# Graph layers on one core: exponents of the ranked layer overwrite their masks, and elementwise work is placed by an estimate of each engine's backlog

## Chip, core and metric

The kernel runs on one core of a Trainium2 chip. The metric is the time of one execution on the device, in microseconds (us). Five engines run side by side, each with its own queue of instructions that it works off in order: TensorE (PE, matrix products), VectorE (DVE), ScalarE (ACT), GpSimd (POOL) and SyncE (SP, here only for issuing DMAs). PEld is TensorE's loading of weights.

## What is computed

Node features x (3327 x 64) pass four layers with one sparse weighted adjacency matrix adj (3327 x 3327); each layer adds its result to x. Cut to what matters:

```python
def layer0(h):                       # twice: k = 0, 1
    m = adj @ (x @ W); gi = m @ wih.T + bih; gh = x @ whh.T + bhh
    r = sigmoid(i_r + h_r); z = sigmoid(i_z + h_z); n = tanh(i_n + r * h_n)
    return relu((1 - z) * n + z * x)
def layer1(h):                       # k = 2, the ranked layer
    mask = (adj != 0); rank = cumsum(mask, axis=1); deg = rank[:, -1:]
    kk = minimum(deg, 100); pos = rank - (deg - kk)
    w = mask * where(pos > 0, 0.5 ** (kk - pos), 0)
    return w @ (h @ weight) + bias
def layer2(h):                       # k = 3, 4, 5, the squared ones: w = adj * adj
    for W, b in ...: x = (w @ x) @ W.T + b
def layer3(h):                       # k = 6, 7
    for W in ...: x = tanh(concat([adj @ x, x]) @ W)
# each layer: h = relu(layernorm(x)); x = x + layer(h)
```

## The kernel before

**Products.** There are eight passes over the adjacency matrix, k = 0 to 7 (KIND, line 69: plain, plain, ranked, squared three times, plain twice). The nodes are laid out in two halves of 13 blocks of 128, both halves side by side (64 features each) in the 128 rows of a result. The 13 blocks make four chunks of destination nodes, of 384, 384, 384 and 512 columns, and two groups: group 0 is chunks 0 and 1, group 1 is chunks 2 and 3. A tile is the strip of the transposed matrix of one block of 128 sources and one group: 2 x 768 or 2 x 896 float32 columns, 768 or 896 KB. There are 26 tiles to a group, and they are loaded again for each pair of passes, 234 loads in all (L296 on SP), into NBUF = 20 slots of the on-chip memory.

A unit is (k, chunk, tile): the product of one tile's columns of one chunk with the source block's features y[k], two matmuls side by side (one per half), summed in a bank of PSUM (propagate, L488). In the timeline a float32 unit of 384 columns takes 0.64 us. A ranked unit has bf16 exponents against three bf16 terms of y, so three pairs of matmuls.

**Order.** alone and joint write the list of units (there are 888): joint(g, k) lays pass k of group g and pass k+1 of the same tiles into each other, so that a tile loaded once serves both. In joint(0, 1) the second pass lies 20 tiles behind. The list is not touched by the change. By units: 208 to 263 hold pass 1 of group 0, 250 to 313 the ranked pass of group 0, 314 to 389 that of group 1, with pass 3 (squared in place in the slot) laid in from 326 on.

run (L593) walks this list once and writes out the program of every engine: it issues loads up to 60 units ahead while slots are free (reserve of 3), calls prepare up to PREPARE units ahead, calls expand two units ahead, then propagate. take and give hand out PSUM banks: four for sums, four for everything else.

**The ranked layer.** For each tile a mask (adj != 0, bf16) is written by DVE in two pieces, one per half (L354), into half a slot (class Mask, two masks to a slot). The mask's last row is replaced by the counts behind this block, by a small DMA that POOL issues (L359). The slot of the tile is free again once the mask is made and pass k = 1 has used it. A product with a triangle of constants (tri, L202) then gives each entry's rank as the exponent of a power of two, in PSUM; an eviction turns it into the bits of a bf16 number: on ACT (L404) or on DVE (L402), by a rule of tile, half and group. The exponents land in a tile "e" of three buffers, in expand, two units before use. Counting units (k = -1, L424) in pass 0 give the counts; their masks are made the same way.

**Tasks.** What follows a chunk's last unit of a pass is a generator: evacuation of the sums (L627 on ACT or L629 on DVE), GRU gates (L703 to L721), transposes, residual (L683), layernorm (L664 to L679, with one power on POOL, L675), splitting in three terms (in_three, L742 and L744, then small DMAs on POOL, L751). Each yield names a planned time; spend, called by each unit with its own planned time, counts it down and resumes the generator. finish runs a generator to its end at once. more_constants is such a task, too: it loads weights, builds block-diagonal ones (L147) and multiplies two of them together (L175 to L182). In after_1, evacuation, the relu of the GRU and the layernorm's square are put on ACT (busy=True).

**Squares.** square (L329) sends two of three to ACT (L331), the others to DVE (L333); for passes 3 and 4 in place, up to 6 units ahead, for pass 5 into half a slot at expansion.

Of the kernel before, what the change touches and what calls it, by code (L numbers as in the profile page):

```python
# [14 lines left out]
AX = mybir.AxisListType  # L15

# [27 lines left out]
P = 128  # L44
# [26 lines left out]
NBUF = 20  # L71
LOAD = 60
PREPARE = {COUNT: 6, PLAIN: 6, RANKED: 44, SQUARED: 6}
EXPAND = 2
RESERVE = 3
SPECIAL = None
# [12 lines left out]
def kernel(  # L89
# [9 lines left out]
    nc = tc.nc  # L99

# [35 lines left out]
    def more_constants():  # L136
# [8 lines left out]
        for h in range(2):  # L145
            hs = slice(h * D, (h + 1) * D)
            nc.vector.tensor_copy(bd[hs, :, hs], packed[hs])  # L147
# [14 lines left out]
        for i, (bi, bh) in enumerate(((BI1, BH1), (BI2, BH2))):  # L162
            nc.vector.tensor_add(bsum[:, i], bcol[:, bi:bi + 2], bcol[:, bh:bh + 2])

        nc.vector.tensor_scalar(wide[0:D], wide[0:D], bcol[0:D, BL1:BL1 + 1], None, op0=ALU.add)
# [3 lines left out]
        nc.vector.tensor_copy(brow[:, 3], ps[:, :D])  # L169
        give(i)  # L170

        for wt, ih in ((W1, IH1), (W2, IH2)):
# [4 lines left out]
            nc.scalar.copy(tr, ps[:, :P])  # L177
# [4 lines left out]
            nc.vector.tensor_copy(bd[:, ih:ih + 3, :].rearrange("p g f -> p (g f)"), ps[:, :3 * P])  # L182
# [14 lines left out]
    def mm(out, lhsT, rhs, start=True, stop=True):  # L197


        for h in range(2):  # L200
            hs = slice(h * D, (h + 1) * D)
            nc.tensor.matmul(out[hs], lhsT[:, hs], rhs, start=start, stop=stop)  # L202

# [40 lines left out]
    def advance(c):  # L244
        running.add(c)
        try:
            tasks[c][1] = next(tasks[c][0])
# [32 lines left out]
    class Tile:  # L280

        def __init__(self, q, g, in_place, early=False):
            self.q, self.g, self.in_place, self.early, self.uses = q, g, in_place, early, 0
            self.b0 = CH[GROUPS[g][0]][0]
            self.w = sum(width(c) for c in GROUPS[g])
            self.slot = self.mask = None
            self.squares = set()
# [5 lines left out]
        def load(self):  # L293
            self.slot = dead.popleft()
# [15 lines left out]
    class Mask:  # L310

        def __init__(self, w):
# [6 lines left out]
            self.view = both[:, h * 2 * GWM:h * 2 * GWM + 2 * w].rearrange("p (s w) -> p s w", s=2)  # L319

# [8 lines left out]
    def square(sq, v, turn):  # L329
        if turn % 3:  # L330
            nc.scalar.activation(sq, v, AF.Square)  # L331
        else:
            nc.vector.tensor_tensor(sq, v, v, ALU.mult)  # L333

    def prepare(k, c, t):

        if t is SPECIAL:
            return
        kind = KIND[k] if k != COUNT else COUNT
        if kind in (RANKED, COUNT) and t.mask is None:  # L340
            make_mask(t, kind)
        if kind == SQUARED and t.in_place and c not in t.squares:
            t.squares.add(c)
            square(t.view(c), t.view(c), t.q + c)

    pieces = deque()

    def make_mask(t, kind):

        t.mask = Mask(t.w)  # L350
        rows = P - 1 if kind == RANKED else P

        def piece(half):
            nc.vector.tensor_scalar(t.mask.view[:rows, half], t.view()[:rows, half], 0.0, None, op0=ALU.not_equal)  # L354
            if half == 0 and kind == RANKED:

                for ch in GROUPS[t.g]:
                    finish(("count", ch))
                nc.gpsimd.dma_start(out=t.mask.view[P - 1:P], in_=totals[t.g][t.q:t.q + D + 1:D, :])  # L359
            if half == 1:  # L360
                t.used()

        pieces.extend([(t, 0, piece), (t, 1, piece)])

    def mask_pieces(n=0, t=None):

        while pieces and (n > 0 or any(u is t for u, _, _ in pieces)):
            _, half, piece = pieces.popleft()
            piece(half)
            n -= 1  # L370

    def expand(k, c, t):
# [9 lines left out]
        if KIND[k] == PLAIN or (KIND[k] == SQUARED and t.in_place):  # L382
            return t.view(c)
        if KIND[k] == SQUARED:
            room = Mask(t.w)
# [520 lines left out]
```

## Time and profile before

| | us |
|---|---|
| median of 3 runs | 751.74 |
| lowest, highest | 749.52, 751.97 |
| the profiled execution, its own time | 749.97 |
| its span, first to last instruction | 748.3 |
| PE busy | 706.1 |
| DVE, ACT, POOL busy | 328.5, 239.3, 90.3 |
| evictions of exponents: ACT L404, DVE L402 | 147 x 0.600, 61 x 0.613 |
| mask pieces, DVE L354 | 208 x 0.605 |
| squares: ACT L331, DVE L333 | 138 x 0.887, 70 x 1.021 |
| loads of tiles | 234, 199.7 MB in all |

How to read it: the span lies inside the profiled execution's own time, 1.7 us shorter. A row "out<-in xcount | busy, mean ns" gives the time in which at least one of the group ran and the mean length of one. Matmuls overlap in pairs, so the mean of one is not its share of PE's time. In the slices of section 2 of the page, the span is cut in 40 pieces of 18.7 us, and a digit is the busy share in tenths. A line of waits reads: engine, what waited, for whom, total us, times, longest. L202 is the helper mm, which all dense products, transposes and triangle products share. The granted clock was full in the whole span.

### The profile page before, as it was taken

To read this page: it belongs to the slowest core of one execution; us is meant where nothing else is said; L and a number is where in the kernel's file an instruction comes from. 1 tells how busy PE (TensorE), PEld (TensorE's weight loads), DVE (VectorE), ACT (ScalarE), POOL (GpSimd) and SP (SyncE) were. 2 spreads that over 40 slices of the span, in tenths; PEclk is the share of its full clock that TensorE was granted. 3 is DMA by queue.
4 is the path that set the end of the run, shared out by engine and by line. 5 is a ranking of instruction groups with operands and counts; after the bars stand their busy time and mean duration, and the time that the engine had idled before them with its cause. 6 is when DMAs were issued, how large, how long until landed. Compare 5 with 4: busy or idle time off the path is not lost.

```text
span 748.3 us, 12340 instructions
## 1 busy us (share of the span) xinstructions
PE 706.1 (94%) x5072; PEld 352.8 (47%) x5072; DVE 328.5 (44%) x557; ACT 239.3 (32%) x373; POOL 90.3 (12%) x112
## 2 busy tenths in 40 slices
PE   5979999999988699899899999999999999999997
PEld 2734444343445577555434444334344454344443
DVE  6656646313993877777865113421252510000000
ACT  0002000202135676768659312730055401000000
POOL 4200000001492431312120000000010000000000
PEclk9999999999999999999999999999999999999999
DMA  9999994299486266292699839962977399907990
GB/s 348 401 342 405 405 395 178 85 331 342 133 277 231 100 198 209 89 356 94 217 332 389 313 95 401 405 266 94 385 275 260 140 406 405 395 18 246 397 391 24
DMA packets 67364, 201.54 MB, mean 269 GB/s; under 512 B 6172, under 2 KB 6916, under 8 KB 67308
## 3 DMA queue, kind: packets, MB, share of 16 engines
q1 hardware_dynamic: 64556, 199.70, 72.2%
q8 instruction: 40, 0.66, 0.4%
q10 hardware_dynamic: 576, 0.85, 0.3%
q0 software_dynamic: 2176, 0.20, 0.2%
q14 instruction: 16, 0.13, 0.0%
HBM read 199.68 MB, written 0.85 MB: 268 GB/s over the span
## 4 chain that ended last, share of the span: by engine, by line
PE 49%; DVE 2%; ACT 1%; POOL 1%; issue 0%; ACTq 0%; DVEq 0%; POOLq 0%
PE sum L488 45%; PE temp L202 4%; ACT adj L331 1%; DVE adj L354 1%; POOL st L675 1%; DVE adj L333 0%; DVE y L679 0%; DVE st L664 0%; DVE xs L683 0%; DVE e L402 0%; DVE st L673 0%; DVE t L672 0%; ACT t L627 0%; DVE t L666 0%; DVE xs L839 0%
## 5 line engine op out<-in xcount | busy, mean ns | idle before, releaser
L488 PE MATMUL sum<-adj,y 128*64 128x384 f32 (+1 forms) x2912 | 537.3, 515 | 17.6 <-DVE y L679 9.2
L488 PEld LDWEIGHTS sum<-adj,y 128*64 128x64 f32 x2912 | 214.8, 138 | 277.1 <-issue 240.8
L354 DVE TENSOR_SCALAR adj<-adj 128x768 bf16<-128x768 f32 (+3 forms) x208 | 115.6, 605 | 34.1 <-PE temp L424 29.6
L331 ACT ACTIVATE adj<-adj 128x768 f32<-128x768 f32 (+1 forms) x138 | 112.9, 887 | 52.0 <-PE sum L488 32.4
L333 DVE TENSOR_TENSOR adj<-adj 128x768 f32<-128x768 f32 (+1 forms) x70 | 69.2, 1021 | 54.7 <-DMA adj<-in_adjT 30.2
L404 ACT ACTIVATE e<-temp,bitsb 128x384 int16<-128x384 f32 (+1 forms) x147 | 81.0, 600 | 30.8 <-PE temp L202 11.9
L629 DVE COPY t<-sum 128x384 f32<-128x384 f32 x14 | 7.8, 556 | 181.9 <-PE sum L488 181.9
L488 PE MATMUL sum<-e,adj 128*64 128x384 bf16 (+1 forms) x624 | 73.9, 339 | 4.6 <-DVE e L402 4.3
L202 PE MATMUL temp<-adj,tri 128*64 128x384 bf16 (+1 forms) x416 | 61.0, 341 | 13.2 <-DVE e L402 6.7
L675 POOL TENSOR_TENSOR st<-st,mhalf 128x6 f32<-128x6 f32 (+1 forms) x16 | 27.4, 1712 | 309.6 <-DVE st L674 309.6
L488 PEld LDWEIGHTS <-adj 128*64 128x64 bf16 x624 | 42.7, 110 | 21.3 <-issue 7.4
L402 DVE TENSOR_SCALAR e<-temp 128x384 int16<-128x384 f32 (+1 forms) x61 | 37.2, 613 | 29.8 <-PE temp L202 22.6
L627 ACT COPY t<-sum 128x384 f32<-128x384 f32 (+1 forms) x18 | 9.5, 527 | 113.0 <-PE sum L488 113.0
L202 PEld LDWEIGHTS <-tri 128*64 128x64 bf16 x416 | 30.6, 109 | 31.0 <-issue 19.1
L359 POOL DMA_DIRECT2D adj<-totals x52 | 31.0, 598 | 115.9 <-DVE adj L354 76.2
L424 PE MATMUL temp<-adj,behind 128*64 128x384 bf16 x208 | 27.7, 339 | 1.7 <-DVE adj L354 1.7
L202 PE MATMUL temp<-bd,t 128*64 128x128 f32 (+1 forms) x320 | 26.1, 279 | 0.4 <-ACT t L627 0.4
L655 ACT COPY hT<-temp 128x384 f32<-128x384 f32 (+1 forms) x12 | 6.1, 506 | 59.2 <-PE temp L202 59.2
L424 PEld LDWEIGHTS <-behind 128*64 128x64 bf16 x208 | 14.2, 110 | 20.5 <-issue 18.2
L202 PEld LDWEIGHTS temp<-bd,t 128*64 128x64 f32 x320 | 19.6, 137 | 7.7 <-issue 3.0
L709 DVE SCALAR_TENSOR_TENSOR adj<-temp,bcol,adj 128x384 f32<-128x384 f32 (+1 forms) x8 | 5.2, 650 | 39.7 <-PE temp L202 34.3
L202 PE MATMUL temp<-t,bd 128*64 128x384 f32 (+1 forms) x96 | 21.1, 517 | 0.1
(74 smaller groups left out, 267.7 us busy)
## 6 DMA issues: line engine op xcount, KB each, us to landing
adj<-in_adjT SPq DMA_DIRECT2D x130, 768.0 KB, 8.4
adj<-in_adjT SPq DMA_DIRECT2D x104, 896.0 KB, 11.0
adj<-in_weights SPq DMA_DIRECT2D x2, 352.0 KB, 15.7
xs<-in_x SPq DMA_DIRECT2D x1, 640.0 KB
out<-xs ACTq DMA_DIRECT2D x3, 192.0 KB
adj<-totals POOLq DMA_DIRECT2D x26, 3.0 KB, 3.2
adj<-totals POOLq DMA_DIRECT2D x26, 3.5 KB, 2.3
out<-xs ACTq DMA_DIRECT2D x1, 256.0 KB, 5.9
```

The lines of the kernel that those rows point to most:

```text
L202: nc.tensor.matmul(out[hs], lhsT[:, hs], rhs, start=start, stop=stop)
L331: nc.scalar.activation(sq, v, AF.Square)
L333: nc.vector.tensor_tensor(sq, v, v, ALU.mult)
L354: nc.vector.tensor_scalar(t.mask.view[:rows, half], t.view()[:rows, half], 0.0, None, op0=ALU.not_equal)
L359: nc.gpsimd.dma_start(out=t.mask.view[P - 1:P], in_=totals[t.g][t.q:t.q + D + 1:D, :])
L402: nc.vector.tensor_scalar(wide[:, s], ps[:, :w], BITS, 0.0, op0=ALU.add, op1=ALU.max)
L404: nc.scalar.activation(wide[:, s], ps[:, :w], AF.Relu, bias=bitsb)
L424: nc.tensor.matmul(counts[c][1][s * D:(s + 1) * D, :w], behind[:, NQ - 1 - t.q:NQ - 1 - t.q + D], t.mask.view[:, s, t.cols(c)], start=firs ...
L488: nc.tensor.matmul(acc[h * D:(h + 1) * D, :w], yq[h], rhs[h], start=first and n == 0, stop=last and n == len(terms) - 1)
L627: nc.scalar.copy(m, acc[1][:, :width(c)])
L629: nc.vector.tensor_copy(m, acc[1][:, :width(c)])
L675: nc.gpsimd.tensor_tensor(st[:, 3, :n], st[:, 2, :n], mhalf[:, :n], ALU.pow)
```

## The change

It does these things:
- Exponents are written over the mask that they come from (weigh), and the mask's half slot is freed after its second ranked unit. The tile "e" is gone, and there are 21 slots.
- Three planned clocks, of PE, DVE and ACT, are kept while the program is written out: each matmul adds to PE's, each elementwise instruction on DVE or ACT adds an estimate to its engine's. The backlog of an engine is how far its clock is ahead of PE's.
- Units up to 56 ahead are put in two lists (enqueue): masks, and ready (exponents and in-place squares). Before each unit, fill makes what is due (counting masks 3 units, ranked masks 9, exponents and squares 4 before use) and, if the backlog allows, one more mask piece and one more entry of ready.
- Squares, exponents and evacuations go to the engine with the smaller backlog.
- A task's planned delay grows by the larger backlog, less 0.6 us.
- In after_1, chunks 2 and 3 (late) have three operations of the GRU and two of the layernorm on POOL; relu and square of chunks 0 and 1 go to DVE.
- after_0 first finishes more_constants.

The other edits (vector and scalar in place of nc.vector and nc.scalar, which only count the time) are left out here:

```diff
-NBUF = 20
+NBUF = 21
 LOAD = 60
-PREPARE = {COUNT: 6, PLAIN: 6, RANKED: 44, SQUARED: 6}
+AHEAD = 56
 EXPAND = 2
 RESERVE = 3
+PE, DVE, ACT = range(3)
...
+    clock = [0.0, 0.0, 0.0]
+    def charge(engine, us):
+        clock[engine] = max(clock[engine], clock[PE]) + us
+    def behind_pe(engine):
+        return max(0.0, clock[engine] - clock[PE])
+    def cost(engine, n, small=False):
+        return 0.2 + 0.00095 * n if engine == ACT else 0.04 + (0.0006 if small else 0.00135) * n
...
+                charge(self.key, cost(self.key, n))
+                return getattr(self.engine, name)(*args, **kw)
...
+        clock[PE] += rhs.shape[1] / 2400 * (1 if rhs.dtype == BF16 else 4)
...
-            tasks[c][1] = next(tasks[c][0])
+            us = next(tasks[c][0])
+            tasks[c][1] = us + max(0.0, max(behind_pe(DVE), behind_pe(ACT)) - 0.6)
...
+            self.slot, self.since = dead.popleft(), clock[PE]
...
-    def square(sq, v, turn):
-        if turn % 3:
-            nc.scalar.activation(sq, v, AF.Square)
+    def square(sq, v):
+        n = v.shape[1] * v.shape[2]
+        if behind_pe(ACT) + cost(ACT, n) < behind_pe(DVE) + cost(DVE, n):
+            scalar.activation(sq, v, AF.Square)
         else:
-            nc.vector.tensor_tensor(sq, v, v, ALU.mult)
-    def prepare(k, c, t):
-        if t is SPECIAL:
+            vector.tensor_tensor(sq, v, v, ALU.mult)
+    masks, ready = [], []
+    def enqueue(j):
+        k, c, t = units[j]
+        if k == COUNT:
+            masks.append((j, t, COUNT))
+        elif t is SPECIAL:
+            pass
+        elif KIND[k] == RANKED:
+            if c == GROUPS[t.g][0]:
+                masks.append((j, t, RANKED))
+            ready.append((j, weigh, c, t))
+        elif KIND[k] == SQUARED and t.in_place and c not in t.squares:
+            t.squares.add(c)
+            ready.append((j, square_in_place, c, t))
+        begun = int(bool(masks) and masks[0][1].mask is not None)
+        masks[begun:] = sorted(masks[begun:], key=lambda m: m[0])
+        ready.sort(key=lambda r: r[0])
+    def mask_piece():
+        _, t, kind = masks[0]
+        if t.mask is None:
+            t.mask = Mask(t.w)
+        half = t.mask.pieces
+        t.mask.pieces += 1
+        rows = P - 1 if kind == RANKED else P
+        charge(DVE, cost(DVE, t.w, small=True))
+        nc.vector.tensor_scalar(t.mask.view[:rows, half], t.view()[:rows, half], 0.0, None, op0=ALU.not_equal)
+        if half == 0 and kind == RANKED:
+            for c in GROUPS[t.g]:
+                finish(("count", c))
+            nc.gpsimd.dma_start(out=t.mask.view[P - 1:P], in_=totals[t.g][t.q:t.q + D + 1:D, :])
+            t.since = clock[PE]
+        if half == 1:
+            t.used()
+            masks.pop(0)
+    def weigh(c, t):
+        if c in t.weights:
             return
-        kind = KIND[k] if k != COUNT else COUNT
-        if kind in (RANKED, COUNT) and t.mask is None:
-            make_mask(t, kind)
-        if kind == SQUARED and t.in_place and c not in t.squares:
-            t.squares.add(c)
-            square(t.view(c), t.view(c), t.q + c)
-    pieces = deque()
-    def make_mask(t, kind):
-        t.mask = Mask(t.w)
-        rows = P - 1 if kind == RANKED else P
-        def piece(half):
-            nc.vector.tensor_scalar(t.mask.view[:rows, half], t.view()[:rows, half], 0.0, None, op0=ALU.not_equal)
-            if half == 0 and kind == RANKED:
-                for ch in GROUPS[t.g]:
-                    finish(("count", ch))
-                nc.gpsimd.dma_start(out=t.mask.view[P - 1:P], in_=totals[t.g][t.q:t.q + D + 1:D, :])
-            if half == 1:
-                t.used()
-        pieces.extend([(t, 0, piece), (t, 1, piece)])
-    def mask_pieces(n=0, t=None):
-        while pieces and (n > 0 or any(u is t for u, _, _ in pieces)):
-            _, half, piece = pieces.popleft()
-            piece(half)
-            n -= 1
+        t.weights.add(c)
+        while t.mask is None or t.mask.pieces < 2:
+            mask_piece()
+        w = width(c)
+        for s in range(2):
+            i, ps = take()
+            v = t.mask.view[:, s, t.cols(c)]
+            mm(ps[:, :w], tri, v)
+            if behind_pe(ACT) + cost(ACT, w) < behind_pe(DVE) + cost(DVE, w) + 0.1:
+                scalar.activation(v.bitcast(I16), ps[:, :w], AF.Relu, bias=bitsb)
+            else:
+                vector.tensor_scalar(v.bitcast(I16), ps[:, :w], BITS, 0.0, op0=ALU.add, op1=ALU.max)
+            give(i)
+        spend(STREAM_US * w / CWM * 0.5)
+    def square_in_place(c, t):
+        while t.ranked and (t.mask is None or t.mask.pieces < 2):
+            mask_piece()
+        square(t.view(c), t.view(c))
+    def make():
+        _, f, c, t = ready.pop(0)
+        f(c, t)
+    def fill(i, loaded):
+        while masks and masks[0][0] <= i + (3 if masks[0][2] == COUNT else 9):
+            mask_piece()
+        while ready and ready[0][0] <= i + 4:
+            make()
+        if masks and masks[0][2] == RANKED:
+            t = masks[0][1]
+            room = t.mask is not None or len(spare) > 0 or len(dead) > (0 if t.uses == 1 else RESERVE)
+            short = loaded < i + 14 and t.uses == 1
+            if room and (short or (behind_pe(DVE) < 0.5 and clock[PE] - t.since > 9.0)):
+                mask_piece()
+        if ready:
+            _, f, c, t = ready[0]
+            if f is weigh:
+                able = t.mask is not None and t.mask.pieces == 2 and clock[PE] - t.since > 5.0
+            else:
+                able = clock[PE] - t.since > 9.0 and (not t.ranked or (t.mask is not None and t.mask.pieces == 2))
+            if able and min(behind_pe(DVE), behind_pe(ACT)) < 0.4:
+                make()
...
-        if KIND[k] == PLAIN or (KIND[k] == SQUARED and t.in_place):
+        if KIND[k] == RANKED:
+            return t.mask.view[:, :, t.cols(c)]
...
-        wide = work.tile([P, 2, CWM], I16, name="e", bufs=3)[:, :, :w]
-        mask_pieces(t=t)
-        for s in range(2):
-            i, ps = take()
-            mm(ps[:, :w], tri, t.mask.view[:, s, t.cols(c)])
-            own = chunk_of(t.q % NB) in GROUPS[t.g]
-            busy = any((k - 1, ch) in sums for ch in GROUPS[t.g])
-            if s and (own if t.g == 0 and (own or busy) else c == GROUPS[t.g][1]):
-                nc.vector.tensor_scalar(wide[:, s], ps[:, :w], BITS, 0.0, op0=ALU.add, op1=ALU.max)
-            else:
-                nc.scalar.activation(wide[:, s], ps[:, :w], AF.Relu, bias=bitsb)
-            give(i)
-        spend(STREAM_US * w / CWM * 0.5)
-        if c == GROUPS[t.g][1]:
-            t.mask.free()
-        return wide.bitcast(BF16)
...
+                t.left -= 1
+                if t.left == 0:
+                    t.mask.free()
...
-        if t is not SPECIAL and t.early and t.mask is None:
-            make_mask(t, RANKED)
+        clock[PE] += w / 2400 * (3 if KIND[k] == RANKED else 4)
...
-            while prepared < loaded and prepared < i + PREPARE[KIND[units[prepared][0]] if units[prepared][0] != COUNT
-                                                               else COUNT]:
-                if prepared > i + PREPARE[PLAIN] and not spare and len(dead) <= RESERVE + 1:
-                    break
-                prepare(*units[prepared])
-                prepared += 1
+            for j in range(i, min(len(units), i + AHEAD)):
+                if j not in seen and (units[j][2] is SPECIAL or units[j][2].slot is not None):
+                    seen.add(j)
+                    enqueue(j)
+            fill(i, loaded)
...
-            if k != 2:
-                mask_pieces(1 + len(pieces) // 6)
-            elif not (c in GROUPS[0] and (t is SPECIAL or chunk_of(t.q % NB) in GROUPS[0])):
-                mask_pieces(1)
...
-        if c % 2 or busy:
-            nc.scalar.copy(m, acc[1][:, :width(c)])
+        if behind_pe(ACT) <= behind_pe(DVE):
...
+        e = nc.gpsimd if late else vector
+        e.tensor_tensor(xc[:, :n], v, st[:, 1, :n, None].to_broadcast([P, n, D]), ALU.subtract)
         yield 1.5 * pace
         sq = work.tile([P, 8, D], F32, name="t2")
-        if busy:
-            nc.scalar.activation(sq[:, :n], xc[:, :n], AF.Square)
-        else:
-            nc.vector.tensor_tensor(sq[:, :n], xc[:, :n], xc[:, :n], ALU.mult)
-        nc.vector.tensor_reduce(st[:, 2, :n], sq[:, :n], AX.X, ALU.add)
-        nc.vector.tensor_scalar(st[:, 2, :n], st[:, 2, :n], 1.0 / D, EPS, op0=ALU.mult, op1=ALU.add)
+        e.tensor_tensor(sq[:, :n], xc[:, :n], xc[:, :n], ALU.mult)
+        if late:
+            yield 2.5
...
-        nc.vector.tensor_tensor(d, hT, r, ALU.subtract)
-        nc.vector.tensor_tensor(d, d, z, ALU.mult)
-        nc.vector.tensor_tensor(d, d, r, ALU.add)
+        e = nc.gpsimd if late else vector
+        e.tensor_tensor(d, hT, r, ALU.subtract)
+        e.tensor_tensor(d, d, z, ALU.mult)
+        e.tensor_tensor(d, d, r, ALU.add)
+        if late:
+            yield 4.0
         o = features(c)
-        if busy:
-            nc.scalar.activation(o, d, AF.Relu)
-        else:
-            nc.vector.tensor_scalar(o, d, 0.0, None, op0=ALU.max)
+        vector.tensor_scalar(o, d, 0.0, None, op0=ALU.max)
         dead.append(at)
...
     def after_0(c, acc):
+        finish(NC)
...
-        pace = 1.0 if c in GROUPS[0] else 1.2
-        h2T = yield from gru(acc, c, hT[c], IH2, HH2, BI2, BH2, 1, pace, busy=True)
+        late = c in GROUPS[1]
+        pace = 1.2 if late else 1.0
+        h2T = yield from gru(acc, c, hT[c], IH2, HH2, BI2, BH2, 1, pace, late)
```

## The prediction

> **What bounds the kernel now.** I read the page's busy line and slices first, then busy time by stage, then TensorE's own waits, then the chain of waits, and last the start of every matmul in the timeline.
>
> ```profile
> PE 706.1 (94%) x5072; PEld 352.8 (47%) x5072; DVE 328.5 (44%) x557; ACT 239.3 (32%) x373; POOL 90.3 (12%) x112
> PE   5979999999988699899899999999999999999997
> DVE  6656646313993877777865113421252510000000
> ACT  0002000202135676768659312730055401000000
> ```
>
> TensorE (PE) is the bound on average, with two holes: the first four slices, and slices 11 to 19 (about 206 to 374 us), where VectorE (DVE) and ScalarE (ACT) are both high. Cutting there:
>
> ```profile
> core 0: us, PE busy (x) PEld busy (x) DVE busy (x) ACT busy (x) POOL busy (x), PEclk, DMA share, GB/s
> 0.00:75.00 75.00, 60.23 (x436) 34.70 (x438) 47.33 (x95) 8.87 (x16) 11.60 (x22) 1.00 1.00 374
> 178.60:213.60 35.00, 34.87 (x231) 15.70 (x228) 28.25 (x53) 7.09 (x13) 18.14 (x25) 1.00 0.60 205
> 213.60:289.20 75.60, 63.38 (x660) 46.51 (x661) 53.68 (x106) 45.88 (x88) 29.08 (x32) 1.00 0.59 200
> 289.20:370.30 81.10, 71.78 (x660) 45.55 (x655) 61.68 (x100) 60.37 (x99) 20.04 (x27) 1.00 0.54 191
> 370.30:540.00 169.70, 169.68 (x1044) 72.34 (x1046) 56.36 (x69) 68.72 (x87) 3.80 (x2) 1.00 0.79 295
> ```
>
> Stage 0 to 75 us has DMA at share 1.00: it is bound by loads. The layers after 370 us have PE full. The two rows between are the ranked layer (k = 2) of group 0 and of group 1. Who PE waits for in 213.6 to 392 us:
>
> ```profile
> PE temp L202 <- DVE e L402: 6.7, 6, 2.3
> PE sum L488 <- DVE e L402: 4.3, 2, 2.5
> PE sum L488 <- DMA adj<-in_adjT: 2.6, 1, 2.6
> PE temp L202 <- ACT e L404: 2.5, 2, 1.8
> PE temp L202 <- DMA adj<-totals: 1.8, 1, 1.8
> PE sum L488 <- DVE y L679: 1.2, 1, 1.2
> ```
>
> The exponents (L402, L404), made two units before use, end 13.5 of these us; one wait is for a tile's load. "Busy" hides part of the loss, so I counted work by start times: undisturbed, a plain unit takes 0.64 us (384 columns) or 0.85 (512), a ranked one 0.48 or 0.64, the triangle product of a ranked unit 0.32 or 0.43. Times the counts of the groups: plain units 505, ranked 54 (and 1.5 for the special ones), triangle 36, counting 18, dense and transposes 71, together 686 us. So 62 us of the 748.3 are lost: 20.5 before 75, 2 to 213.6, **16.7 in 213.6 to 289.2, 12.5 in 289.2 to 370.3**, 4 to 600, 6.5 after (3.3 of it the tail). At most some 29 us lie where the change works.
>
> [...] while 18 mask pieces (L354) ran back to back from 214.7 us, the lasty DMA issued at 215.1 took 8.24 us on POOL against some 0.5 us for its sisters. [...] the trace has 995 ns (L689, GpSimd) against 558 (L717, VectorE) for 384 columns, 1.8x.
>
> **The change, part by part.**
>
> *Exponents in the mask, up to 56 units ahead.* The same 208 evictions (147 on ACT at 600 ns, 61 on DVE at 613) and 416 triangle matmuls remain; only their place moves. What goes is the waiting: PE need not stand behind an eviction of two units ago. Is there room? In 178.6 to 370.3 us DVE is busy 143.6 us and ACT 113.3, 257 of 383. If 20 us of PE idling go, it is 257 of 343, 75%, and before unit 250 ACT has 7.1 of 35 us in use. Space: a ready tile costs the half slot that its mask held anyway (until its second use in place of its second expansion, some 0.5 to 1 us longer); 21 slots instead of 20 pay for that. So of 29.2 lost us I keep these:
> - 178.6 to 231.7: a load at 223.1 us that waited for slots which late masks held (2.6 us of wait; DVE busy 19.6 of the 20 us from 200 to 220). Masks can start some 14 units earlier now. Left: 1 of 4.4 (bounds 0 and 4.4).
> - to 289.2: 12.3 lost. Here the next limit is the chain of chunks 0 and 1 (GRU, layernorm, three terms): begun at 224.0 and 231.5 us, its last step (L744) ends near 262 and 266, some 38 and 34 us in the jam. Its own instructions add up to some 20 us with their handovers. PE's cover from unit 259 to 288 is 4 plain units (2.6), 24 ranked ones (11.5) and dense work (9), 23 us, or with group 1's triangle products 25 or more. Left: 3 (0 to 8).
> - 289.2 to 357: 8.7 lost. In-place squares (L331 0.89, L333 1.02 us) no longer stand ahead of an eviction that is due. Left: 4 (2 to 8).
> - 357 to 370.3: 3.8 lost. The chain after k = 2 of chunk 2 runs from L629 at 357.9 to y at 370.3, 12.4 us; the evictions and a square that cut into it on DVE (0.69, 1.22, 0.68 us) go, so some 9.5 are left. But PE's cover shrinks as well, since the triangle products go ahead of it: units 383 to 391 are 8 x 0.64 + 0.85 + 0.64 dense, 6.6 us. Left: 2.9 (2 to 4).
> Sum left 10.9 of 29.2: **minus 18.3 us**.
>
> *Engine by estimated backlog.* The estimate gives 0.565 us for a 384-wide ACT pass (trace 0.580) and 0.558 for DVE (0.556), a mask piece 0.50 (0.598); reduces are charged for 6 outputs, 0.05 us against 0.552, so DVE is fuller than it thinks by 1 us per layernorm. Good enough to split evenly. The squares that PE waited for at 551.8 and 593.2 us (0.65 and 0.5) should go: **minus 1** (0 to 1.5).
>
> *Late chunks on GpSimd.* Five elementwise operations of each of chunks 2 and 3 after k = 1: 5 x 0.995 + 5 x 1.378 = 11.9 us on POOL for 6.2 us off DVE; relu and square leave ACT (0.5 to 0.6 each). These chunks end at 167.9 and 178.6 us and are needed at unit 250 (213.6) and 272 (246.8), so 35 us of plain units hide the longer chain, even with the added 4.0 and 2.5 us: **0**. Behind them in POOL's queue stand the last-row DMAs of the masks; that is a rival below.
>
> *A task's delay grows by the backlog; finish(NC) in after_0.* This one costs. The first layernorms charge DVE some 8 us before PE's clock moves, so the weights' DMAs come at planned 12.3 us instead of 5, the copies L147 at 32.3 instead of 25, and after their 3.9 charged us the next step is due at about 39. after_0 of chunk 0 comes at about 38.7 planned us and flushes the rest in one go: products of 0.1, 0.22 + 0.64 and 0.22 + 0.64, with two waits for an ACT copy (some 0.8 us each with the hand-overs). Today this is at 50 to 56 us, under the loads (DMA share 1.00); then it stands at 63 us, after the last tile of group 0 has come in (62.3), where nothing hides it: 1.8 + 1.6 = **plus 3.4** (0 to 5). The brow DMA it also issues waits for nothing on SP. Counting masks are made 3 units ahead, not 6; they wait only for tiles that landed long before: 0 (up to 2).
>
> *One more slot.* Before 75 us DMA is full, so it brings nothing there; later it is counted above.
>
> Sum: 748.3 - 18.3 - 1 + 3.4 = 732.4 us of span. The profiled execution took 749.97, 1.7 more than its span, and the median is 1.8 above that: 732.4 + 1.7 + 1.8 = 735.9; I say **736**.
>
> **The rivals.**
> - *Half:* the chains set the pace, not the exponents. Chains lengthen where DVE does masks first, and the tasks' delays grow by backlog. For it: a 38 us chain today. Against it: most of that is waiting behind evictions. With 8 left in 231.7 to 289.2 and 8 in 289.2 to 357 the gain falls by 9: 745.
> - *It cannot run ahead:* slots. At unit 250 about 24 masks hold 12 slots, open tiles, terms and a GRU some 6. If only a tile or two of exponents fit ahead, today's waits stay, minus perhaps 4 from the even split, plus 3.4: 751. Against it: exponents need no space beyond the mask, and the order of units has some 20 tiles wait with their masks today.
> - *Slower: early triangle products stop PE.* They now stand in PE's queue in front of plain units, on a planned 5 us after the mask's first piece. The last row comes by a GpSimd DMA: issue 0.54 to 0.99 us, landing 1.6 to 6.1 us, behind POOL's new 11.9 us of elementwise work[...]. If real POOL lags the plan, every such product stops work that was ready. The point: my gain of 15.9 over 52 tiles is used up at 0.31 us of wait per tile; at 0.55 us per tile (28 us) it ends at 764. Against it: today only 1.8 us of PE wait is for this DMA, and pieces now come at most one per unit.
>
> **Numbers.** Forecast 736 (729 to 742): 0.54. Half, 745 (742 to 749): 0.22. No effect, 751: 0.09. Slower, 764: 0.15. Between runs about 0.3% (2.3 us) can be told from no change. Faster 0.77, same 0.08, slower 0.15. The range starts below the forecast's lower bound, 726, and reaches into the no-effect case, 751.
>
> **What would show it.** Right: waits of PE for e in 213 to 370 us nearly gone; exponents spread back over 165 to 213 us; that stretch some 18 us shorter; PE waiting for y or the three terms instead; a new stall of about 3 us near 63 us, with L177's ACT copies there. Wrong: PE waiting for the totals DMA in many places; tile loads that come later in 230 to 340 us; or chains of chunks 0 and 1 still over 30 us.

## The result and the profile after

| us | before | after |
|---|---|---|
| median (runs, lowest to highest) | 751.17 (4, 749.52 to 751.97) | 767.79 (4, 767.3 to 768.07) |
| profiled execution: own time, span | 749.97, 748.3 | 767.95, 766.3 |
| mean granted clock in it | 1.000 | 0.986 |

The changed kernel is slower: 1.0223 times the time before, 95% interval 1.0204 to 1.0243. 736 was forecast, with a range up to 751.

The page's busy line and slices after the change (a slice is now 19.2 us):

```profile
PE 714.8 (93%) x5072; PEld 351.8 (46%) x5072; DVE 330.8 (43%) x552; ACT 236.9 (31%) x368; POOL 96.7 (13%) x122
PE   5979999999988868889989999999999999999997
DVE  6645636421493676777886412510063620000000
ACT  0002100302254446567884503641043501000101
PEclk9999999999999989999999999999999999999999
```

The number of matmuls is the same, 5072, but they are busy 8.7 us longer, and PEclk has an 8: PE itself ran slower for a while. The hole in PE's slices is still there, in slices 11 to 20 (counted from 0). Now busy time by stage. I cut at the starts of the same units as before: unit 78 (74.3 us), 208 (184.5), 250 (225.3), 314 (306.9), 392 (387.9).

```profile
core 0: us, PE busy (x) PEld busy (x) DVE busy (x) ACT busy (x) POOL busy (x), PEclk, DMA share, GB/s
0.00:74.30 74.30, 57.56 (x410) 31.51 (x412) 45.54 (x91) 7.14 (x12) 11.59 (x22) 0.98 1.00 373
184.50:225.30 40.80, 38.03 (x270) 18.45 (x268) 24.72 (x45) 13.20 (x24) 23.16 (x27) 1.00 0.41 137
225.30:306.90 81.60, 65.91 (x632) 41.49 (x629) 52.30 (x102) 42.95 (x82) 25.69 (x35) 0.94 0.55 204
306.90:387.90 81.00, 72.33 (x636) 43.77 (x630) 63.76 (x106) 58.42 (x92) 22.30 (x28) 0.96 0.49 163
```

Units 250 to 313 take 81.6 us (75.6 before) and get a clock of 0.94. In units 208 to 249 DVE has only 24.7 of 40.8 us in use (28.3 of 35.0 before) and DMA moves 137 GB/s (205 before): both have room, and yet too little is prepared. Who PE waits for in 225 to 410 us:

```profile
PE sum L563 <- ACT adj L125: 8.0, 5, 2.9
PE temp L231 <- DMA adj<-totals: 6.0, 5, 2.3
PE temp L231 <- DVE adj L125: 3.8, 2, 3.6
PE temp L231 <- DVE adj L398: 3.2, 3, 2.7
PE sum L563 <- DMA adj<-in_adjT: 3.1, 3, 1.5
```

L563 is the sums' matmul (L488 before), L231 the helper mm (L202), L125 every recorded operation of DVE and ACT, L398 a mask piece (L354). The waits for exponents, 13.5 us before, are down to the third line. In their place PE waits for the three terms of chunks 0 and 1 (first line, units 288 and 300; at 392 it is ACT's squares), for the last row and the pieces of masks (second and fourth) and for loads.

By the prediction's own count, PE has 686.1 us of work at full clock in both kernels; it loses 62.2 us before and 80.2 after. The 18.0 us lie here:

| units | before, lost us | after, lost us |
|---|---|---|
| 0 to 77 | 20.6 | 24.3 |
| 78 to 207 | 1.2 | 3.5 |
| 208 to 263 | 5.2 | 9.4 |
| 264 to 313 | 12.2 | 19.1 |
| 314 to 391 | 12.5 | 14.0 |
| 392 to 887 | 10.4 | 10.0 |

Inside these sums are six stretches of 3.41 us at half the clock, 1.7 us of lost work each, up to 10.2 us in all; five lie in units 208 to 391. The profiled execution before had none (the last 0.8 us of the one and 0.5 us of the other apart, which are at half clock too; on all this, the last section).

### The profile page after: what moved, and what is told of

Read it like the earlier page. It is cut to its first block, busy times and chain, and to the rows that moved or that the text cites. A ratio compares the mean times of both kernels' runs of the same rounds, so it can differ in the third digit from the quotient of the medians.

```text
span 766.3 us, 12377 instructions
## 1 busy us (share of the span) xinstructions
PE 714.8 (93%) x5072; PEld 351.8 (46%) x5072; DVE 330.8 (43%) x552; ACT 236.9 (31%) x368; POOL 96.7 (13%) x122
## 4 chain that ended last, share of the span: by engine, by line
PE 78%; DMA 8%; DVE 7%; issue 2%; SPq 2%; POOL 1%; ACT 0%; DVEq 0%; POOLq 0%; ACTq 0%
PE sum L563 64%; PE temp L231 13%; DMA adj<-in_adjT 4%; DMA adj<-in_weights 2%; DVE adj L398 2%; SPq L328 2%; DVE adj L125 2%; PE temp L494 2%; DVE st L125 1%; DMA adj<-totals 1%; DVE y L125 1%; POOL st L745 1%; DVE t L125 1%; DVE xs L125 1%; POOL adj L403 0%
## 5 line engine op out<-in xcount | busy, mean ns | idle before, releaser
L563 PE MATMUL sum<-adj,y 128*64 128x384 f32 (+1 forms) x2912 | 536.8, 517 | 21.8 <-DMA adj<-in_adjT 16.7
L563 PEld LDWEIGHTS sum<-adj,y 128*64 128x64 f32 x2912 | 212.9, 138 | 281.9 <-issue 236.8
L398 DVE TENSOR_SCALAR adj<-adj 128x768 bf16<-128x768 f32 (+3 forms) x208 | 118.7, 624 | 38.1 <-PE temp L494 35.1
L125 ACT ACTIVATE adj<-adj 128x768 f32<-128x768 f32 (+1 forms) x126 | 105.9, 897 | 46.6 <-DMA adj<-in_adjT 26.6
L125 ACT ACTIVATE adj<-temp,bitsb 128x384 int16<-128x384 f32 (+1 forms) x152 | 84.2, 613 | 69.0 <-PE temp L231 66.3
L125 DVE TENSOR_TENSOR adj<-adj 128x768 f32<-128x768 f32 (+3 forms) x94 | 86.9, 951 | 40.9 <-DMA adj<-in_adjT 25.8
L125 ACT COPY t<-sum 128x384 f32<-128x384 f32 (+1 forms) x28 | 14.3, 510 | 272.4 <-PE sum L563 272.3
L563 PE MATMUL sum<-adj,adj 128*64 128x384 bf16 (+1 forms) x624 | 73.6, 353 | 6.0 <-ACT adj L125 5.7
L231 PE MATMUL temp<-adj,tri 128*64 128x384 bf16 (+1 forms) x416 | 58.8, 352 | 15.8 <-DVE adj L125 6.6
L125 DVE TENSOR_TENSOR xs<-xs,y 128x384 f32<-128x384 f32 (+1 forms) x4 | 2.4, 592 | 140.5 <-ACT y L125 140.5
L563 PEld LDWEIGHTS <-adj 128*64 128x64 bf16 x624 | 41.8, 114 | 23.6 <-ACT adj L125 6.9
L125 DVE TENSOR_SCALAR adj<-temp 128x384 int16<-128x384 f32 (+1 forms) x56 | 32.3, 588 | 36.7 <-PE temp L231 30.9
L231 PEld LDWEIGHTS <-tri 128*64 128x64 bf16 x416 | 27.6, 112 | 42.4 <-issue 21.6
L403 POOL DMA_DIRECT2D adj<-totals x52 | 34.6, 666 | 37.2 <-ACT adj L125 26.4
L231 PE MATMUL temp<-bd,t 128*64 128x128 f32 (+1 forms) x320 | 26.0, 279 | 1.3 <-ACT t L125 0.8
L125 ACT COPY hT<-temp 128x384 f32<-128x384 f32 (+1 forms) x12 | 6.1, 506 | 65.6 <-PE temp L231 65.6
L231 PEld LDWEIGHTS temp<-bd,t 128*64 128x64 f32 x320 | 19.5, 137 | 7.6 <-issue 3.3
L231 PE MATMUL temp<-hT,bd 128*64 128x384 f32 (+1 forms) x96 | 22.0, 519 | 0.0
L125 DVE TENSOR_TENSOR y<-temp,brow 128x384 f32<-128x384 f32 (+1 forms) x8 | 4.7, 589 | 40.0 <-PE temp L231 40.0
```

The lines of the kernel that those rows point to most:

```text
L125: return getattr(self.engine, name)(*args, **kw)
L563: nc.tensor.matmul(acc[h * D:(h + 1) * D, :w], yq[h], rhs[h], start=first and n == 0, stop=last and n == len(terms) - 1)
```

## The experiments

Two theories, both seen in the trace. **Late masks**: fill makes at most one early mask piece per unit, only if there is room, and only under a DVE backlog of 0.5 us and 9 planned us after the tile's slot was taken or its first piece made. (The exception, short, lifts the last two conditions for a tile with no other use left, but only while fewer than 14 units are loaded ahead; e1 drops that 14.) A tile without its mask keeps a whole slot, so loads come late, so later masks have no room: all last-row DMAs of group 0's masks are issued by 229.4 us before, by 286.7 after; the first load of group 1 by 217.7 and 255.1. Here are the mask pieces in units 208 to 249 and 250 to 263, before (L354, two lines), after (L398, two lines) and in e1 below (L398, two lines):

```profile
178.60:213.60 35.00, 15.39 (x29) 1.00 0.60 205
213.60:231.70 18.10, 10.14 (x22) 1.00 0.83 284
184.50:225.30 40.80, 13.07 (x20) 1.00 0.41 137
225.30:246.90 21.60, 3.91 (x8) 0.92 0.40 146
184.90:231.30 46.40, 27.40 (x38) 1.00 0.57 190
231.30:247.50 16.20, 4.19 (x8) 1.00 0.44 168
```

(The second number is DVE's time on them, with their count; a piece on a border counts twice.) Of the 52 pieces of group 0, all are finished by the start of unit 264 before, 29 after and 47 in e1.

**Grown delays**: what follows chunks 0 and 1 after k = 1 becomes a slower chain, since each of its steps waits longer by the backlog: from evacuation to the last term 38.2 and 34.2 us before, 40.4 and 48.9 after. Here are the beginnings and ends of these chains, first before (ACT's evacuations of chunks 0 and 1, then the last terms on DVE), then after the change (ACT's evacuation of chunk 0, DVE's of chunk 1, then the last terms on DVE):

```profile
224.03 0.48 ACT L627 COPY t<-sum 128x384 f32<-128x384 f32 x1 [6.12 <-PE sum L488]
231.54 0.48 ACT L627 COPY t<-sum 128x384 f32<-128x384 f32 x1
261.69 0.55 DVE L744 TENSOR_TENSOR adj<-y,adj 128x384 bf16<-128x384 f32 x1
265.16 0.55 DVE L744 TENSOR_TENSOR adj<-y,adj 128x384 bf16<-128x384 f32 x1
```

```profile
237.55 0.48 ACT L125 COPY t<-sum 128x384 f32<-128x384 f32 x1 [1.62 <-PE sum L563]
...
246.66 0.56 DVE L125 COPY t<-sum 128x384 f32<-128x384 f32 x1
277.40 0.56 DVE L125 TENSOR_TENSOR adj<-y,adj 128x384 bf16<-128x384 f32 x1 [0.58 <-ACT adj L125]
295.00 0.56 DVE L125 TENSOR_TENSOR adj<-y,adj 128x384 bf16<-128x384 f32 x1 [0.58 <-ACT adj L125]
```

The rivals were GpSimd (the late chunks), the place of the exponents itself, and the start. Ratios are to the kernel before, run beside each of them (medians of 751.1 to 751.9). Idle times of PE are the profile's.

**e1: masks first.**
```diff
-            short = loaded < i + 14 and t.uses == 1
+            short = t.uses == 1
```


> The changed kernel, with one rule changed: a ranked mask piece is made as soon as its tile has no other use left, instead of only when VectorE's planned backlog is under 0.5 us or loads run short. Theory M (late masks hold whole slots, so tiles load late, and each long stall of TensorE is followed by some 3.4 us at half clock): the loads of group 0's last four tiles are issued before 220 us again (223.7 to 229.1 in the changed kernel), group 1's first loads before 240 us (255.1), fewer stretches at half clock than the 6, and the time is 755 to 761 us. Theory P (the elementwise work on GpSimd delays the masks' last rows): no change, 766 to 769. Theory D (the task delays and the flush of the constants): no change, 766 to 769.


Measured 749.45, ratio 0.9969 [0.9954, 0.9984]: 18 us faster than the changed kernel and below the range expected. Group 0's last-row DMAs are all issued by 237.4, its last mask piece ends at 250.2 (287.8 in the changed kernel), group 1's loads begin at 229.2, exponents stand up to 42 units ahead (27 in the changed kernel), units 208 to 391 take 184.5 us in place of 203.4. So making masks first is enough to take the loss away. The chains of chunks 0 and 1 shorten with it, to 33.6 and 35.8 us, though the delays still grow: late masks did part of their harm through these chains. Which of the two dropped conditions (the backlog or the 9 us) held the masks back, no run tells.

**e2: nothing on GpSimd.**
```diff
-        late = c in GROUPS[1]
-        pace = 1.2 if late else 1.0
+        late = False
+        pace = 1.2 if c in GROUPS[1] else 1.0
```


> The changed kernel without work of GRU and layernorm on GpSimd: chunks 2 and 3 after k = 1 go to VectorE as well. Theory M: VectorE has 6 us more to do in 170 to 215 us and masks come no earlier: 766 to 771 us. Theory P: the waits of TensorE for the masks' last rows (6.0 us) and what hangs on them go: 757 to 762. Theory D: no change, 766 to 769.


Measured 768.6, ratio 1.0226 [1.0181, 1.0271]: no gain. The five operations of the late chunks on GpSimd are not the cause.

**e3: delays as planned.**
```diff
-            tasks[c][1] = us + max(0.0, max(behind_pe(DVE), behind_pe(ACT)) - 0.6)
+            tasks[c][1] = us
```


> The changed kernel with the tasks' planned delays as in the kernel before, without the backlog added. Theory D: the flush of the constants near 63 us is gone (3 to 5 us) and the chains after each pass are shorter: 755 to 760 us. Theory M: only the start is better, 763 to 766. Theory P: as M, 763 to 766.


Measured 750.23, ratio 0.9986 [0.9967, 1.0004]: 17.6 us faster than the changed kernel and again below the range expected, though three waits for loads at units 257 to 259 remain (0.3, 1.8 and 0.8 us). No wait for terms is left at 288 or 300. So this line, too, is enough to make the difference.

**e8 and e9: where the delays do harm.** A unit counter turns the growth on from unit 208 (e8) or off from there (e9).
```diff
-            tasks[c][1] = us + max(0.0, max(behind_pe(DVE), behind_pe(ACT)) - 0.6)
+            tasks[c][1] = us
+            if here[0] >= 208:
+                tasks[c][1] += max(0.0, max(behind_pe(DVE), behind_pe(ACT)) - 0.6)
```


> The changed kernel, with tasks' delays as planned up to unit 207 and grown by the backlog from unit 208 on. Theory (the grown delays harm inside the ranked stage, where the chains of chunks 0 and 1 run): units 208 to 392 still take some 200 to 204 us, PE still waits for the terms at units 288 and 300, and only the start gains (unit 208 near 182.3 in place of 184.5), so 763 to 766. Rival (the harm is done earlier: by unit 208 the planner has fewer free slots, and that decides how late the masks come): 750 to 755, units 208 to 392 some 189 us.

> The changed kernel, with tasks' delays grown by the backlog up to unit 207 and as planned from unit 208 on. Theory (harm inside the ranked stage): units 208 to 392 take some 188 to 191 us, no wait for the terms at units 288 and 300, unit 208 near 184.5 as in the changed kernel, so 751 to 755. Rival (harm done earlier): 764 to 768.


Measured 767.08, ratio 1.0216 [1.0188, 1.0244], for e8 and 751.48, ratio 0.9998 [0.9985, 1.0011], for e9: e8 ends 1 us above the range expected, e9 inside it. The harm of this line is done inside the ranked stage: nearly all 16 us. In e9 the same chains look so (ACT's evacuation of chunk 0, DVE's of chunk 1, last terms):

```profile
235.84 0.48 ACT L125 COPY t<-sum 128x384 f32<-128x384 f32 x1 [1.34 <-PE sum L566]
...
243.70 0.56 DVE L125 COPY t<-sum 128x384 f32<-128x384 f32 x1
264.79 1.91 DVE L125 TENSOR_TENSOR adj<-y,adj 128x384 bf16<-128x384 f32 x1
271.15 0.54 DVE L125 TENSOR_TENSOR adj<-y,adj 128x384 bf16<-128x384 f32 x1
```

235.8 to 266.7 and 243.7 to 271.7: 30.9 and 28.0 us, where e8 has 39.1 and 48.8. The last-row DMAs of group 0 end nearly as late in e9 (279.1 us) as in the changed kernel (286.7); the early chains alone take most of the jam away.

**e5 and e6: both together.** e5 is e1 with e3; e6 also makes counting masks 9 units ahead.
```diff
-        while masks and masks[0][0] <= i + (3 if masks[0][2] == COUNT else 9):
+        while masks and masks[0][0] <= i + 9:
```

> e1 and e3 together: masks as soon as their tile is free otherwise, and tasks' delays without the backlog. Each alone brought 17 to 18 us. If both act on the same stalls (late chains and late tiles, each with its half-clock stretches), little is added: 743 to 749 us. If they were independent causes it would be near 732. No wait for the three terms at unit 288 and no wait for loads at units 257 to 259.

> e5 with counting masks up to 9 units ahead of use instead of 3. If the start lost its time to counting masks that stand behind the constants' copies (3.8 us of wait at 49 us in e3), unit 78 starts 3 to 5 us earlier than in e5 and the time is 739 to 745. If the start is bound by loads alone, no change against e5.


Measured 744.51, ratio 0.9910 [0.9891, 0.9929], and 744.36, ratio 0.9904 [0.9880, 0.9929]: both faster than before, e6 by 0.7 to 1.2%. The counting masks gain nothing that can be told: the wait for them at 49.2 us (2.9) gives way to one for a layernorm's t at 50.4 (2.8). As a square, in us: changed 767.8, without late masks 749.5, without grown delays 750.2, without both 744.5. Taking away either gains 18, both 23: they act largely on the same stalls.

**e4: exponents late again, on e1.** 
```diff
-            if able and min(behind_pe(DVE), behind_pe(ACT)) < 0.4:
+            if able and f is not weigh and min(behind_pe(DVE), behind_pe(ACT)) < 0.4:
```


> As e1, and exponents are made only 4 units before use, never early. Theory M with early exponents worth what the prediction says: 5 to 12 us slower than e1, 760 to 770. If early exponents are worth nothing, or cost VectorE time that the masks need: equal to e1 or faster.


Measured 755.84, ratio 1.0058 [1.0041, 1.0074]: 6.4 us more than e1. That is what running ahead is worth when masks are in time (and the delays grow).

**e7: writing in place alone.** The kernel before, with the exponents written over the mask and 21 slots; distances and engines as before. ACT's eviction is changed as DVE's is.
```diff
-NBUF = 20
+NBUF = 21
...
-            mm(ps[:, :w], tri, t.mask.view[:, s, t.cols(c)])
+            v = t.mask.view[:, s, t.cols(c)]
+            mm(ps[:, :w], tri, v)
...
-                nc.vector.tensor_scalar(wide[:, s], ps[:, :w], BITS, 0.0, op0=ALU.add, op1=ALU.max)
+                nc.vector.tensor_scalar(v.bitcast(I16), ps[:, :w], BITS, 0.0, op0=ALU.add, op1=ALU.max)
```


> The kernel before with one part of the change: exponents overwrite their masks (the mask is given back after the second ranked unit), no tile e, 21 slots; all distances and engines as before. Prediction: this part alone moves waits little, 748 to 752 us. If the longer life of the mask costs slots that matter, slower, 753 to 758; if the 21st slot matters, 744 to 748.


Measured 749.72, ratio 0.9976 [0.9966, 0.9985]: a gain of 1.8 us. The load wait of 2.6 us at unit 259 is gone (units 250 to 263 lose 1.5 us in place of 4.4).

**e10 and e11: what is left in e6.** e10 has exponents and squares due 8 units before use (4) and ranked masks 12 (9); e11 makes early entries only when both engines are free. First e10's edit, then e11's:
```diff
-        while masks and masks[0][0] <= i + 9:
+        while masks and masks[0][0] <= i + (9 if masks[0][2] == COUNT else 12):
...
-        while ready and ready[0][0] <= i + 4:
+        while ready and ready[0][0] <= i + 8:
...
-            if able and min(behind_pe(DVE), behind_pe(ACT)) < 0.4:
+            if able and max(behind_pe(DVE), behind_pe(ACT)) < 0.4:
```


> The kernel of e6 (masks first, plain delays, counting masks 9 units ahead), with exponents and squares due 8 units before use in place of 4, and ranked masks due 12 in place of 9. What is left of stalls from unit 316 on (3.7 at unit 317, 1.2 at 327 and at 347, about 6 us in all) comes where exponents are made only when due, 5 units ahead. If the due time is what sets that lead, the lead becomes 9 and most of it goes: 739 to 742. If the slots set it (no slot is free, so a mask that is due sooner only delays a load), nothing is gained or it is slower: 744 to 750.

> The kernel of e6 with early exponents and squares made only when both planned backlogs are under 0.4 us, not when one of them is. In units 208 to 250 of e6 PE loses 6.4 us, nearly all of it in triangle products that wait for an eviction on VectorE that stands behind mask pieces. If those early products are the price of running ahead and the condition lets them in too soon, most of the 6.4 us go and nothing returns later: 738 to 741. If the exponents are then simply missing ahead of units 264 to 314 (where e6 loses 4.1 us in all), the stalls come back there: 744 to 750.


Measured 753.34, ratio 1.0036 [1.0019, 1.0053], and 747.24, ratio 0.9951 [0.9937, 0.9965]; both worse than e6. In e10 the lead from unit 322 on did become 9, and the stalls moved instead of going: 4.4 us at unit 323 and 2.8 at 357, both for the last-row DMA, so earlier only meant standing before a mask that was not complete. In e11 the small waits of units 208 to 248 went, as the first theory said, but one wait of 7.1 us came at unit 249. PE, ACT and DVE of e11 there:

```profile
223.37 1.00 PE L231 MATMUL temp<-adj,tri 128*64 128x384 bf16 x4 [7.14 <-ACT adj L125]
...
222.22 0.62 ACT L125 CAST adj<-y 128x512 bf16<-128x512 f32 x1 [4.79 <-DVE y L125]
222.74 1.99 ACT L125 ACTIVATE adj<-temp,bitsb 128x384 int16<-128x384 f32 x4
...
216.81 3.05 DVE L398 TENSOR_SCALAR adj<-adj 127x768 bf16<-127x768 f32 x4
219.77 1.60 DVE L125 TENSOR_TENSOR adj<-y,adj 128x384 bf16<-128x384 f32 x1
221.30 0.16 DVE L125 TENSOR_SCALAR st<-st 128x8 f32<-128x8 f32 x1
221.49 0.69 DVE L125 SCALAR_TENSOR_TENSOR y<-t,st 128x512 f32<-128x512 f32 x1
```

Read upwards from DVE: four mask pieces and a subtraction, then chunk 3's scale, then its y at 221.5. ACT's first copy of that y had been queued and sat idle for 4.8 us; the four evictions stood behind it, and PE behind them. This is the prediction's slower rival in another dress: an early product stops PE through an in-order queue. Whether that chunk's longer chain on GpSimd has a part in it stays open; a run without it was not made.

**c1: stalls of chosen length.** The kernel before, with eight extra stalls of PE in layers that lose nothing else (a product, n passes on DVE over its result, a product of the last); the extra products are not used.
```diff
+    STALLS = {430: 2, 450: 4, 470: 6, 490: 7, 560: 8, 585: 9, 760: 10, 800: 14}
+    def hold(n):
+        i, ps = take()
+        mm(ps[:, :P], ident, ident)
+        pad = work.tile([P, CWM], F32, name="t2")[:, :P]
+        nc.vector.tensor_copy(pad, ps[:, :P])
+        for _ in range(n):
+            nc.vector.tensor_tensor(pad, pad, pad, ALU.mult)
+        mm(ps[:, :P], ident, pad)
+        give(i)
...
+            if i in STALLS:
+                hold(STALLS[i])
```


> The kernel before with eight stalls of TensorE put into its quiet stretches: a product, its copy by VectorE, a chain of 2, 4, 6, 7, 8, 9, 10 and 14 small VectorE operations, and a product that waits for it (some 1.3 to 4.9 us of stall each, 24 us in all). The rest of the computation is unchanged. If stalls from about 2.6 to 3 us on are followed by some 3.4 us at half clock, the longest four or five show it, each costing 1.7 us beyond its length: 782 to 785 us. If the half clock has another cause: none, and 775 to 777.


One run, 789.85 us, span 788.1, clock 0.978: above the range expected. Five of the eight stalls are followed by half clock, though not the five longest, and four more stretches at half clock (from 22.4, 240.8, 261.3 and 305.7 us) lie outside the stalls put in. Read in the last section.

## Why the prediction was wrong, point by point

**The bound and the count** held: work is 686.1 us in both, and the change moved time only where it was expected to act, in units 0 to 391. That at most 29.2 us lay there was not put to the test: e6, the best version, gained 10.7 us of it (units 208 to 391 take 181.0 us, 191.7 before, both profiles at full clock).

**Exponents ahead, minus 18.3: the step that failed.** It took the masks for settled and asked only for room on DVE and in the slots. "Masks can start some 14 units earlier now": the first piece comes 3 units earlier (at unit 202, before at 205), but the second at unit 222 in place of 207, and the last one of group 0 ends 57 us later (230.8 before, 287.8 after). The prediction counted on about 24 masks at unit 250; 10 of group 0 are finished there (15 before). When unit 264 starts, it is 26 before, 14 after, 23 in e1. Not DVE's capacity set their pace:

```profile
178.60:231.70 53.10, 49.98 (x338) 24.15 (x336) 40.01 (x77) 14.41 (x27) 33.44 (x38) 1.00 0.68 232
```
```profile
184.50:246.90 62.40, 56.55 (x403) 27.98 (x400) 34.56 (x64) 23.96 (x45) 28.81 (x35) 0.97 0.41 140
```

The first line is the kernel before, the second after, both units 208 to 263: DVE busy (x77 and x64) fell from 40.0 of 53.1 us to 34.6 of 62.4, and DMA from 232 to 140 GB/s. I had read DVE at 19.6 of 20 us and asked only whether it had room, not whether the new gate lets it work; e1, which opens that gate, gains 18.3 us. "Space: a ready tile costs the half slot that its mask held anyway" held in e7, but the tiles that lack a mask hold whole slots, and those grew in number (from none to 12 at unit 264). The one direct price of running ahead is 6.4 us (e4 against e1), a third of the 18.3. The losses left against the sum:

| units | left, predicted | after | e6 |
|---|---|---|---|
| 208 to 263 | 1 | 9.4 | 6.7 |
| 264 to 313 | 3 | 19.1 | 3.8 |
| 314 to 391 | 4 + 2.9 | 14.0 | 8.6 |

Where masks are in time and delays plain (e6), the second row comes out near the 3 predicted and the third 1.7 above the 6.9. The first was mis-sized even there: 6.4 of the 6.7 us fall in units 208 to 249, where triangle products of units to come start some ten times 0.4 to 1.2 us late, waiting for a bank that DVE or ACT has not yet emptied; DVE's evictions stand behind mask pieces there. So even e6, with 744.4 us, stays above the range of the forecast, 729 to 742.

**Grown delays, plus 3.4: right where I looked, missed where it mattered.** The flush stands where it was put. PE after the last tile of group 0 has come in:

```profile
63.00 0.28 PE L231 MATMUL temp<-ident,t 128*64 128x64 f32 x4
63.12 0.39 PE L231 MATMUL temp<-ident,bd 128*64 128x128 f32 x4
63.87 0.87 PE L231 MATMUL temp<-bd,t 128*64 128x384 f32 x4 [0.36 <-ACT t L125]
64.57 0.39 PE L231 MATMUL temp<-ident,bd 128*64 128x128 f32 x4
65.49 0.87 PE L231 MATMUL temp<-bd,t 128*64 128x384 f32 x4 [0.53 <-DVE bd L125]
66.16 0.53 PE L494 MATMUL temp<-adj,behind 128*64 128x384 bf16 x4
```

63.0 to 66.2 is 3.2 us, forecast 3.4. Two waits for chunks' y at 88.3 and 158.5 us (0.7 each) come on top, not foreseen. Yet plain delays alone don't win this time back: in e3 and e8 units 0 to 77 lose 24.0 and 24.9 us, since PE then waits 3.6 us near 50 us for a counting mask; with these masks made earlier too (e6) they lose 20.8. But the same line inside the ranked stage is worth some 16 us (e8 against e9). The working treated it as a cost of the start and named chains that lengthen only in the rival Half, at 9 us. The backlog is presumably largest while exponents are made early (no run shows the planned backlog itself); in any case the change slows the chain that it then leaves as the limit.

**Engine by backlog, minus 1: right.** The stage of k = 5 (units 628 to 731) loses 0.7 us in place of 2.0.

**Late chunks on GpSimd, 0: right** for this kernel (e2 can't be told from it).

**Counting masks, 0 (up to 2): right** for this kernel, where PE's waits for them sum to 1.6 us (1.7 before); not so with plain delays (e3, above). **One more slot: right**, within e7.

**The rivals.** The slower one ended near the measured time, 764, by another mechanism. It put 0.55 us per tile, an estimate, on the last-row DMA; the waits for it sum to 6.0 us, 0.12 per tile, under its turning point of 0.31. Half had the right mechanism and stopped at 745, since it took the masks for settled. Of the signs of being wrong, two came true in full: the loads of group 1 came later, and both chains stayed over 30 us (40.4 and 48.9).

**The clock** was in no case: half-clock stretches take up to 10.2 of the 18.0 us in the profiled pair.

## What to carry to other kernels

When a change replaces a fixed schedule by conditions, follow each condition through the crowded stage with the real occupancy of slots: an engine with time to spare makes nothing if a gate (here on a planned backlog and on a tile's age) is shut. A rule that delays one kind of work by the backlog of another must be priced where the backlog is largest, above all on the chain that the change itself leaves last. And make first what frees memory (here masks), and only then what merely saves a wait.

## What the runs showed of the hardware

I had not expected PE's clock to halve within a kernel that is over 90% busy. In the traces, each stretch at half clock within a kernel lasts 3.41 us or two or three times that (10.24 us in e2). Their starts lie on a grid: in the profile after, the first of the six is at 55.5 us, and the others start 180.9, 211.6, 221.9, 259.4 and 283.3 us later, that is 53, 62, 65, 76 and 83 times 3.413 us (c1, after the first at 22.4 us: 64, 70, 83, 121, 142 and 150 times). In the 3.41 us of the grid ahead of each of these six, PE was idle for 1.96 to 3.06 us, never throughout. Here are stretches of c1's grid around three of its stalls, of 2.6, 2.9 and 3.6 us (here counted from start to start of PE's products, less the undisturbed step; the profile's idle time is 0.2 us less; PE busy is the second number, PEclk the third from the end):

```profile
432.00:435.40 3.40, 1.05 (x12) 0.56 (x10) 2.69 (x8) 0.00 (x0) 0.00 (x0) 1.00 0.95 348
435.40:438.80 3.40, 3.40 (x14) 1.41 (x12) 3.40 (x5) 0.00 (x0) 0.00 (x0) 0.50 0.07 28
449.00:452.40 3.40, 1.71 (x14) 0.72 (x10) 1.47 (x6) 0.00 (x0) 0.00 (x0) 1.00 0.00 0
452.50:455.90 3.40, 2.51 (x18) 1.28 (x20) 0.77 (x3) 0.74 (x2) 0.00 (x0) 1.00 0.00 0
531.00:534.40 3.40, 0.78 (x8) 0.50 (x10) 2.79 (x9) 0.00 (x0) 0.00 (x0) 1.00 0.00 0
534.40:537.80 3.40, 3.40 (x12) 0.95 (x10) 0.00 (x0) 0.00 (x0) 0.00 (x0) 0.50 0.00 0
```

The stall of 2.9 us lies across two stretches (PE busy 1.71 and 2.51 us of 3.4), and the clock stays at 1.00; the shorter one of 2.6 us lies in one (PE busy 1.05 us), and the next is at 0.50. Counted over the 14 traces of this case, each cut along its own grid, once PE had started: every full-clock stretch with PE idle for more than 2.1 us of 3.4 was followed by half clock (50 of 50), none with less than 1.7 (0 of some 2900); in between both occur (11 of 39). In the two stages of c1 where PE bounds all (units 420 to 627), the stalls sum to 15.4 us, and what PE loses there rose by 21.8 us (from 1.6 to 23.4); the other 6.4 us over four half-clock stretches of 3.41 us are 1.6 us each.

So, of c1's three stalls above, those of 2.6 and 3.6 us were followed by half clock, at some 1.6 us each, and the one of 2.9 us was not: where the stall lay on the grid told there, not its length alone. The kernel before has stalls of that size too (PE idle 2.66, 2.57 and 2.48 us before 46.6, 223.1 and 304.6 us), but in its profile none left PE idle for over 2.0 us within one stretch of the grid, and none was followed by half clock. Of its timed runs, those at a granted clock of 0.997 have a median of 750.0 us, those at 0.990 one of 752.5. Its profiled execution, at 1.000, was a lucky one. e6 was granted between 0.988 and 1.000: its two runs at 0.988 took 745.1 and 746.4 us, the one at 1.000 took 740.6.
